# VectorE in written order through all four groups of layer 1

## The chip, the cores and the metric

The kernel runs on one core of a Trainium2 chip. The metric is the device time of one execution in microseconds (us); lower is better. The core has five engines, each with its own queue that it works through in order: TensorE (PE, matrix products; PEld is its weight load), VectorE (DVE, elementwise work), ScalarE (ACT, functions such as Ln and Exp), GpSimd (POOL) and SyncE (SP, which issues the transfers). They work side by side and wait for one another with semaphores. Which instruction stands ahead of which on one engine is fixed when the kernel is built.

## The reference

Sixteen graphs of 1024 nodes with 64 features share one adjacency matrix. Four layers follow one another, each of them `x = layernorm(x + layer(x))`. The change is in layer 1, which is, for each feature by itself, a softmax average over the neighbours:

```
feat   = softplus(x * (w0 / sqrt(2)) + b0)
scores = feat * wa + ba
attn   = softmax over neighbours j of scores[b, j, d]      # masked by adj
out    = sum over j of attn[b, i, j, d] * feat[b, j, d]
x      = layernorm(x + out)
```

Since a score depends on the neighbour and the feature alone, the average is a quotient of two products with the adjacency matrix: `adj @ (exp(scores) * feat)` over `adj @ exp(scores)`. Layers 0 and 2 are graph attention with one head, layer 3 has four heads; they enter here only where their work lies beside layer 1's.

## The kernel before

The 1024 nodes are eight blocks (`C = 8`) of 128, the graphs four groups (`NG = 4`) of four (`GB = 4`). All node features of a group lie in one SBUF tile, `x0` to `x3`. Layer 1 is a loop over the groups g, and inside it over the eight row blocks ic of the output.

*The product* (`product_l1`, L2008). For one row block TensorE adds up 16 products of 128 by 128 by 512 in one PSUM tile `po`: eight blocks of neighbours, each with a high and a low part (`hi`, `lo`) of the right side, which holds for four graphs both the exponentials and the exponentials times the features. The tiles `po` come from a pool of two buffers (L636), so the product of block n+2 can't start before the last reader of block n has done: L2027.

*The average* (`average`, L2019). ScalarE takes the logarithm of the denominators and the exponential of its negative, which is a first reciprocal `r` (L2022, L2023). VectorE improves it by one step and applies it (L2025, L2026, L2027), subtracts the quotient from `x` (L2030, the signs are turned so that this adds it) and takes the statistics of four rows (four L2032, into `st`). Each of these instructions reads what the one ahead of it wrote.

*The preparation of the next group* (`prep_l1`, L1862). A group has two halves q of two graphs each. Nine tasks are laid on the row blocks of the group before: ScalarE's softplus in four steps (L1870, L1873, L1877, L1880), VectorE's sum (L1883), eight transposes on TensorE (L1888, tile `pf`), VectorE's maximum (L1894, L1895, L1897) and ScalarE's exponential (L1898), eight transposes back (L1908, tile `pe`), then `hi` on ScalarE (L1910, L1916) and on VectorE the weighted features (L1911) and `lo` (L1912, L1917). The second L1917 of a half pair is the last thing that the next group's first product needs.

*The moments* (`moments`, L765). Behind a group's eight averages VectorE makes mean and variance out of `st` in seven rows (L771, 772, 773, 775, 776, 777 and L715, which keeps the largest variance). ScalarE takes the root (L718, L719), VectorE refines it in four rows (L723, 724, 725, 782), and ScalarE scales the group's 32 rows (L791, `scaled`). Root, refinement and scaling are a list `last`, of which the next group's loop runs one entry behind each average: `for task in last[ic : ic + 1] + ahead[ic]`. For group 0 this list holds what layer 0 has left over for its last graphs (L1125, L1130, L1150, L1158, L1163, L1164, L1171, moments, scaling). The list behind group 3 is run in layer 2.

*Layer 2's beginning*. From block 3 of group 2 on, the first tasks of layer 2 lie on the row blocks as well: transposes (L944), small products (L951, L998), and in group 3 eight masked exponentials `e` on VectorE (L1048).

*The order*. The loop is not wrapped in an order for TensorE, ScalarE or VectorE in groups 0 to 2: a planner in the language's layer decides there, by its own costs, how the instructions of an engine follow one another. In group 3 VectorE's instructions are kept in the order in which the program writes them (`tc.manual_schedule`), as those of all engines are in layers 0, 2 and 3.

Of the kernel before, what the change touches and what calls it, by code (L numbers as in the profile page):

```python
# [582 lines left out]
def fast_path(  # L583
# [26 lines left out]
    C = N // P  # L610
# [3 lines left out]
    GB = 4  # L614
    NG = B // GB
# [149 lines left out]
    def moments(st):  # L765


        n = st.shape[1]
        t = {k: small.tile([P, n], F32, tag=f"bn_{k}", name=f"bn_{k}") for k in ("mean", "d", "var", "rstd", "shift")}
        v = nc.vector  # L770
        v.tensor_tensor(t["d"], st[:, :, 1], st[:, :, 4], ALU.subtract)  # L771
        v.tensor_tensor(t["var"], st[:, :, 2], st[:, :, 5], ALU.add)
        v.tensor_tensor(t["mean"], st[:, :, 1], st[:, :, 4], ALU.add)

        v.scalar_tensor_tensor(t["d"], t["d"], 0.25, t["d"], ALU.mult, ALU.mult)
        v.tensor_scalar(t["var"], t["var"], 1.0 / D, LN_EPS, ALU.mult, ALU.add)
        v.tensor_tensor(t["var"], t["var"], t["d"], ALU.add)
        root, step = inverse_root(t["rstd"], t["var"])

        def finish():  # L780
            step()
            v.scalar_tensor_tensor(t["shift"], t["mean"], -0.5, t["rstd"], ALU.mult, ALU.mult)  # L782
            return t["rstd"], t["shift"]

        return root, finish

    def scaled(dst, src, moments, rows):

        rstd, shift = moments
        for c in rows:  # L790
            nc.scalar.activation(  # L791
                dst[:, c, :], src[:, c, :], AF.Identity,
                bias=shift[:, c : c + 1], scale=rstd[:, c : c + 1],
            )
# [1129 lines left out]
    with tc.tile_pool(name="ps_g", bufs=1, space=bass.MemoryType.PSUM, reuse_waits="tile") as ps_g, tc.tile_pool(  # L1924
# [66 lines left out]
        g=lambda: l1["psum"]("pg").rearrange("p (i c) q -> p i (c q)", i=2),  # L1991
# [11 lines left out]
    with tc.tile_pool(name="l1", bufs=2, reuse_waits="tile") as pool:  # L2003
        l1["halves"] = pool
        l1["psum"] = lambda name: ps_l.tile([P, C, P], F32, tag="l", name=name)
        aR = pool.tile([P, C, N], F32R, tag="aR", name="aR", bufs=1)

        def product_l1(g, ic):  # L2008
            po = ps_a.tile([P, 2, 2, P], F32, tag="acc", name=f"po{g}_{ic}")
            for k in range(C):  # L2010
                for e in (his[g], los[g]):
                    nc.tensor.matmul(  # L2012
                        po.rearrange("p q k f -> p (q k f)"), aR[:, k, ic * P : (ic + 1) * P],
                        e[:, k].rearrange("p q k f -> p (q k f)"),
                        start=(k == 0 and e is his[g]), stop=(k == C - 1 and e is los[g]),
                    )
            return po

        def average(g, ic, po, st):  # L2019

            r = pool.tile([P, 2, P], F32, tag="r1", name="r1", bufs=2)
            nc.scalar.activation(r, po[:, :, 1, :], AF.Ln)  # L2022
            nc.scalar.activation(r, r, AF.Exp, scale=-1.0)  # L2023
            t = pool.tile([P, 2, P], F32, tag="t1", name="t1", bufs=1)
            nc.vector.tensor_tensor(t, po[:, :, 1, :], r, ALU.mult)  # L2025
            nc.vector.scalar_tensor_tensor(r, t, 2.0, r, ALU.subtract, ALU.mult)  # L2026
            nc.vector.tensor_tensor(t, po[:, :, 0, :], r, ALU.mult)  # L2027
            y = xg[g][:, ic]
            yf = y.rearrange("p b d -> p (b d)")
            nc.vector.tensor_tensor(yf, yf, t.rearrange("p q f -> p (q f)"), ALU.subtract)  # L2030
            for b in range(GB):
                nc.vector.bn_stats(st[:, ic * GB + b, :], y[:, b, :])  # L2032

        ending[0]()
        for i, task in enumerate([l1_tasks[q][-2 + i] for q in range(2) for i in range(2)]):
            for k in range(2 * i, 2 * i + 2):
                (nc.scalar.copy if k % 2 else nc.vector.tensor_copy)(aR[:, k, :], aT[:, k, :])
            task()
        last = ending[1:]
        for g in range(NG):  # L2040
            ahead = [[] for _ in range(C)]
            for q in range(2 if g + 1 < NG else 0):

                for ic, task in zip((q, q, q, q, q + 1, q + 2, q + 2, q + 4, q + 5), prep_l1(g + 1, q)):
                    ahead[ic].append(task)
            places = {NG - 2: (3, 3, 4, 4, 5, 6, 7, 7), NG - 1: (0, 0, 0, 0, 0, 1, 2, 3, 4, 5, 6, 7)}.get(g, ())
            for ic, task in zip(places, l2_ahead[8 if g + 1 == NG else 0 :]):
                ahead[ic].append(task)
            st = (l1["both"] if g + 1 == NG else pool).tile([P, C * GB, 6], F32, tag="st1", name=f"st{g}")
            with ExitStack() as order:  # L2050
                if g + 1 == NG:
                    order.enter_context(tc.manual_schedule(engines={mybir.EngineType.DVE}))
                for ic in range(C):
                    po = product_l1(g, ic)
                    average(g, ic, po, st)
                    for task in last[ic : ic + 1] + ahead[ic]:
                        task()
            y = xg[g].rearrange("p c b d -> p (c b) d")
            mo = {}

            def spread_of(mo=mo, st=st):
                mo["root"], mo["end"] = moments(st)

            if g + 1 < NG:
                spread_of()

            def root(mo=mo):
                mo["root"]()

            def shift(mo=mo):  # L2070
                mo["n"] = mo["end"]()

            def rows(c, y=y, mo=mo):
                scaled(y, y, mo["n"], range(c * 8, c * 8 + 8))

            last = [spread_of] * (g + 1 == NG) + [root, shift] + [lambda c=c, rows=rows: rows(c) for c in range(C * GB // 8)]
    l3a = None

    def open_l3a():
# [128 lines left out]
    last = [(E, BURSTS + j, outs[E][1][0][3 * j : 3 * j + 3]) for j in range(3)]  # L2208
# [54 lines left out]
def kernel(tc, *args):  # L2263


    nc = tc.nc
    with tc.tile_pool(name="flag", bufs=1) as fp:
        redo = fp.tile([1, 1], I32, tag="redo", name="redo")
        fast_path(tc, redo, *args)
        again = nc.values_load(redo[0:1, 0:1], min_val=0, max_val=1)  # L2270
        with tc.If(again == 1):
            general_path(tc, *args)
# [32 lines left out]
```

## Time and profile before

| | |
|---|---|
| median of three runs | 1922.41 us (1922.39 to 1925.25) |
| the profiled execution's own time | 1922.41 us |
| its span, first to last instruction | 1920.4 us |
| layer 0, with loading | 0 to 265 us |
| hand-over to layer 1 | 265 to 279 us |
| layer 1 (first to last product) | 279 to 419 us |
| layer 2 | 419 to about 610 us |
| layer 3 | about 610 us to the end |
| first L2025 of groups 0, 1, 2, 3 | 287.87, 322.39, 356.90, 393.93 us |
| last L2025 of group 3 | 419.71 us |
| mean granted clock of TensorE | 0.99 |

The profile is taken from one execution. Its page gives the busy time of each engine and its share of the span, then the span in 40 slices with the busy share of each in tenths. A table by stretches gives, for each stretch of the span, busy microseconds and number of instructions of PE, PEld, DVE, ACT and POOL, the granted clock of TensorE (1.00 is full, 0.50 is half), the busy share of the transfer engines and GB/s. A line of waits reads: engine and line that waited, engine and line that ended the wait, microseconds in total, number of times, the longest. A line of the timeline reads: start, duration, engine, line, operation, written tile and read tiles with their shapes, and in brackets how long the engine was idle before it and what released it.

### The profile page before, as it was taken

Reading aid. Unit: us, or ns where it says so; the run is one execution under the profiler, and the core shown is the slowest. Engines: PE = TensorE matmul, PEld = TensorE weight load, DVE = VectorE, ACT = ScalarE, POOL = GpSimd, SP = SyncE. Lnnn points to the kernel's source line nnn. Section 1 sums busy time; section 2 is a strip of 40 time slices with the busy share of each in tenths; the row PEclk is TensorE's granted clock in tenths of the full one; section 3 lists DMA queues with packets and bytes.
Section 4 is the critical chain, followed back from the end, with each engine's and each line's share of the span. In section 5 each row is a group of like instructions: output and inputs, shape, how many; then the busy total and the mean of one; then the engine's idle time right before and its main releaser. Section 6 shows DMA issues by size and latency. Waiting matters only on the chain. (4 is left out here: it accounts for less than half of the span.)

```text
span 1920.4 us, 25705 instructions
## 1 busy us (share of the span) xinstructions
PE 1859.8 (97%) x9505; PEld 764.7 (40%) x9505; DVE 1753.8 (91%) x2924; ACT 1324.7 (69%) x2352; POOL 76.0 (4%) x77
## 2 busy tenths in 40 slices
PE   8999989999998999999999999999999999999996
PEld 4444347763333333333333333333333333333332
DVE  7899988899999888899998998999989899899997
ACT  4566568857879677676767767767676766776764
POOL 0000000000000000000000000000000000000001
PEclk8999989999999999999999999999999999999998
DMA  7000000000000300000001000010000100000000
GB/s 183 1 1 1 1 1 1 1 1 1 1 1 12 89 12 13 23 12 18 12 18 29 12 18 12 18 28 12 18 12 18 29 12 18 12 24 23 12 23 13
DMA packets 45746, 35.87 MB, mean 19 GB/s; under 512 B 37295, under 2 KB 37616, under 8 KB 45614
## 3 DMA queue, kind: packets, MB, share of 16 engines
q1 hardware_dynamic: 43534, 33.64, 6.8%
q8 instruction: 76, 1.25, 0.3%
q10 hardware_dynamic: 2080, 0.52, 0.1%
q14 instruction: 56, 0.46, 0.1%
HBM read 29.45 MB, written 4.70 MB: 18 GB/s over the span
## 5 line engine op out<-in xcount | busy, mean ns | idle before, releaser
L1450 ACT ACTIVATE e<-s,shift 128x1024 f32<-128x1024 f32 x512 | 538.9, 1123 | 240.5 <-PE s L1446 238.6
L1454 DVE TENSOR_TENSOR e<-e,aT 128x1024 f32<-128x1024 f32 x512 | 596.1, 1215 | 5.0 <-ACT e L1450 4.8
L1446 PE MATMUL s<-hT 64*128 64x512 f32 x2048 | 489.3, 602 | 2.5 <-ACT zT L1493 1.4
L1461 PE MATMUL y<-e,vals 128*64 128x512 f32 x2048 | 483.3, 599 | 1.9 <-DVE e L1454 1.0
L1446 PEld LDWEIGHTS s<-hT 64*128 64x128 f32 x2048 | 183.6, 185 | 288.0 <-issue 143.1
L1461 PEld LDWEIGHTS y<-e,vals 128*64 128x64 f32 x2048 | 135.2, 136 | 269.1 <-issue 200.1
L1048 DVE SCALAR_TENSOR_TENSOR e<-G_l,q,aT 128x1024 f32<-128x1024 f32 x150 | 185.7, 1278 | 0.2
L1630 DVE TENSOR_TENSOR e<-e,aT 128x1024 f32<-128x1024 f32 x128 | 156.3, 1225 | 11.2 <-ACT e L1617 1.6
L1060 PE MATMUL y_l<-e,vals_l 128*64 128x512 f32 x608 | 145.5, 605 | 2.3 <-DVE e L1048 2.3
L1622 DVE SCALAR_TENSOR_TENSOR junk<-e,aN 128x1024 bf16<-128x1024 f32 x120 | 146.1, 1217 | 0.0
L1617 ACT ACTIVATE e<-s,shift 128x1024 f32<-128x1024 f32 x128 | 138.6, 1114 | 2.4 <-PE s L1612 2.4
L1612 PE MATMUL s<-h2T 64*128 64x512 f32 x512 | 125.8, 591 | 0.0
L1638 PE MATMUL y<-e,h2v 128*64 128x512 f32 x512 | 125.6, 592 | 0.0
L2012 PE MATMUL po<-hi,aR 128*128 128x512 f32 x256 | 102.3, 400 | 10.5 <-ACT hi L1916 6.7
L1389 POOL PARTITION_ALL_REDUCE gtop<-top x48 | 52.9, 1101 | 1254.3 <-DVE top L1387 1046.9
L2012 PE MATMUL po<-lo,aR 128*128 128x512 f32 x256 | 100.5, 393 | 0.3 <-DVE lo L1917 0.3
L791 ACT ACTIVATE x<-m,bn_shift,bn_rstd 128x64 f32<-128x64 f32 x224 | 77.2, 428 | 15.7 <-DVE bn_shift L782 15.7
L1612 PEld LDWEIGHTS s<-h2T 64*128 64x128 f32 x512 | 50.1, 186 | 60.1 <-issue 37.3
L1493 ACT COPY zT<-poT 64x512 f32<-64x512 f32 x124 | 72.0, 581 | 1.1
L1060 PEld LDWEIGHTS y_l<-e,vals_l 128*64 128x64 f32 x608 | 38.6, 137 | 76.8 <-issue 61.0
L1468 ACT COPY yT<-y 128x512 f32<-128x512 f32 x64 | 38.5, 601 | 43.6 <-PE y L1461 42.6
L1638 PEld LDWEIGHTS y<-e,h2v 128*64 128x64 f32 x512 | 36.6, 137 | 73.6 <-issue 58.5
(299 smaller groups left out, 2144.4 us busy)
## 6 DMA issues: line engine op xcount, KB each, us to landing
r<-inverse SPq DMA_DIRECT2D x62, 256.0 KB
adj<-in_adj_dram SPq DMA_DIRECT2D x16, 512.0 KB
out_dram<-res SPq DMA_DIRECT2D x15, 256.0 KB
x<-in_x_dram SPq DMA_DIRECT2D x14, 256.0 KB
rows<-yT SPq DMA_DIRECT2D x62, 4.0 KB
x<-in_x_dram ACTq DMA_DIRECT2D x2, 256.0 KB
sums<-rows SPq DMA_DIRECT2D x31, 8.0 KB
inverse<-rt SPq DMA_DIRECT2D x31, 8.0 KB
```

Of the source, the lines that this page charges most:

```text
L1048: nc.vector.scalar_tensor_tensor(e, of_pair(b - b % 2, b % 2), pq[b - b % 2][1][:, k, b % 2 : b % 2 + 1], aT[:, k, :], ALU.max, ALU.mult,)
L1060: nc.tensor.matmul(held["y"][h * D : (h + 1) * D, :], vals[b][:, k, :], e[:, h * HALF : (h + 1) * HALF], start=(k == 0), stop=(k == C - 1),)
L1446: nc.tensor.matmul(s[:, i, :], hT[rows, k * P : (k + 1) * P], hT[rows, cols], start=True, stop=True)
L1450: nc.scalar.activation(e, s, AF.Exp, bias=shifts[b, n])
L1454: nc.vector.tensor_tensor(e, e, bc_mid(aT[:, k, h * HALF : (h + 1) * HALF], 2), ALU.mult)
L1461: nc.tensor.matmul(held[h][i * D : (i + 1) * D, :], vals[b][:, k, :], e[:, i, :], start=(k == 0), stop=(k == C - 1),)
L1612: nc.tensor.matmul(s[:, i, :], hT[rows, (i + k // CH) % 2, k % CH * P : (k % CH + 1) * P], hT[rows, 0, :], start=True, stop=True,)
L1617: nc.scalar.activation(e, s, AF.Exp, bias=shifts[b])
L1622: nc.vector.scalar_tensor_tensor(junk.rearrange("p c q -> p (c q)").bitcast(BF16), e.rearrange("p i q -> p (i q)"), 1.0, aN[:, k, :], ALU. ...
L1630: nc.vector.tensor_tensor(e, e, aT[:, k, :].rearrange("p (i q) -> p i q", i=2), ALU.mult)
L1638: nc.tensor.matmul(held["o"][h * D : (h + 1) * D, :], vals["out", b][:, k, :], e[:, h, :], start=(k == 0), stop=(k == C - 1),)
L2012: nc.tensor.matmul(po.rearrange("p q k f -> p (q k f)"), aR[:, k, ic * P : (ic + 1) * P], e[:, k].rearrange("p q k f -> p (q k f)"), start ...
```

## The change

The order that group 3 has is put on all four groups: VectorE's instructions of the whole loop over row blocks stand as the program writes them. And the moments of groups 0 to 2 are no longer written behind their own group. They become the first entry of the list `last`, as they were for group 3, so that they are written behind the first average of the next group, with root, refinement and each scaling one block later than before. No instruction is added or removed.

```diff
             st = (l1["both"] if g + 1 == NG else pool).tile([P, C * GB, 6], F32, tag="st1", name=f"st{g}")
-            with ExitStack() as order:
-                if g + 1 == NG:
-                    order.enter_context(tc.manual_schedule(engines={mybir.EngineType.DVE}))
+            with tc.manual_schedule(engines={mybir.EngineType.DVE}):
                 for ic in range(C):
                     po = product_l1(g, ic)
                     average(g, ic, po, st)
...
             def spread_of(mo=mo, st=st):
                 mo["root"], mo["end"] = moments(st)
 
-            if g + 1 < NG:
-                spread_of()
-
             def root(mo=mo):
                 mo["root"]()
...
-            last = [spread_of] * (g + 1 == NG) + [root, shift] + [lambda c=c, rows=rows: rows(c) for c in range(C * GB // 8)]
+            last = [spread_of, root, shift] + [lambda c=c, rows=rows: rows(c) for c in range(C * GB // 8)]
```

## The prediction

> **What bounds the kernel now.** I read the page first (busy shares, busy tenths), then the busy times by stage, then for layer 1 alone what TensorE waits for, and last VectorE's timeline there. The page, for one execution:
>
> ```profile
> PE 1859.8 (97%) x9505; PEld 764.7 (40%) x9505; DVE 1753.8 (91%) x2924; ACT 1324.7 (69%) x2352; POOL 76.0 (4%) x77
> PE   8999989999998999999999999999999999999996
> DVE  7899988899999888899998998999989899899997
> ```
>
> No engine is the bound everywhere, so the stage decides. Stretches of the span (columns: the stretch, its length, busy us and instructions of PE, PEld, DVE, ACT, POOL, granted clock, DMA): layer 0, its hand-over, layer 1, layer 2, layer 3.
>
> ```profile
> 0.00:265.00 265.00, 257.97 (x1696) 108.25 (x1696) 238.68 (x517) 142.53 (x377) 9.02 (x18) 0.98 0.14 34
> 265.00:279.00 14.00, 5.80 (x44) 5.04 (x40) 11.05 (x22) 13.70 (x24) 0.00 (x0) 0.77 0.01 2
> 279.00:419.00 140.00, 135.81 (x644) 110.12 (x644) 118.79 (x358) 108.98 (x246) 0.35 (x1) 0.99 0.00 1
> 419.00:610.00 191.00, 174.22 (x866) 72.02 (x864) 189.49 (x344) 148.09 (x503) 8.45 (x7) 0.98 0.01 4
> ```
>
> Layer 1 is TensorE's: 135.8 of 140 us, VectorE 118.8. Layer 2 is VectorE's: 189.5 of 191. So a delay of VectorE at the end of layer 1 is passed on whole, but for the 1.5 us that VectorE idles in layer 2. What TensorE waits for from 279 to 419:
>
> ```profile
> PE po L2012 <- DVE t L2027: 2.0, 2, 1.8
> PE po L2012 <- DVE top L1895: 1.8, 1, 1.8
> PE po L2012 <- DVE lo L1917: 0.3, 1, 0.3
> ```
>
> That is 4.1 us, and 3.8 of it (0.2, 1.81 and 1.80, inside the loop over groups) is all that a better order there could win. The end of group 0, on VectorE (start, us, line, operation):
>
> ```profile
> 313.69 0.41 DVE L2025 TENSOR_TENSOR t<-po,r 128x256 f32<-128x256 f32 x1
> 314.02 1.22 DVE L1917 TENSOR_TENSOR lo<-f,hi 128x1024 fp32r<-128x1024 f32 x1
> 315.15 0.42 DVE L2026 SCALAR_TENSOR_TENSOR r<-t,r 128x256 f32<-128x256 f32 x1
> 315.62 1.28 DVE L1894 TENSOR_SCALAR_CACHE_REDUCE t<-pf,wa 128x1024 f32<-128x1024 f32 x1
> 316.82 0.08 DVE L1894 DVE_READ_ACCUMULATOR t<-pf,wa 128x1 f32 x1
> 316.82 0.42 DVE L2027 TENSOR_TENSOR t<-po,r 128x256 f32<-128x256 f32 x1
> ```
>
> The average of row block 6 is taken apart. The last `lo` (L1917), which group 1's first product needs, is slipped in behind its first instruction and ends at 315.24. That product starts at 317.39, held by L2027 of block 6, which frees one of the two PSUM buffers, and not by `lo`.
>
> **What the change moves.** The order of the built program shows each average (L2025, 2026, 2027, 2030, four L2032) as one block. Seven moment rows (L771 to L715) move from the group's end to behind the next group's first average. The last L1917 of a half stands behind the whole of average 6. Instructions and their number stay. The orders of TensorE and ScalarE are planned anew inside layer 1; from layer 2 on all are as before. SP has no DMA in this stage and POOL one reduction for layer 2, whose ScalarE readers are done some 6 us before the first mask that needs them; both cost nothing, and one late reader would cost its lateness.
>
> In written order a group becomes a loop that nothing breaks: first average, VectorE's list up to the last `lo`, first product of the next group, Ln and Exp, first average. Its rows:
>
> 1. An average in one block: the starts 397.56, 398.02, 398.48, 398.94, 399.40 and the next at 399.92 give 2.36. (Mixed with other rows an instruction of it takes 0.34, not 0.46.) Seven of them: 16.5.
> 2. A half's preparation, start to start: L1883 1.14 to 1.19, L1894 with L1895 and L1897 1.62, L1911 1.13, L1912 1.16, L1917 1.15: 6.2. Two: 12.5.
> 3. Group 0 also holds the rest of layer 0: L1125, L1130 and two L1150 1.28, L1163 and L1164 1.33, eight L1171 1.16, seven moment rows 0.89, four step rows 0.73: 5.4.
> 4. Groups 1 and 2 hold instead seven moment rows of 32 columns, 1.2, and four step rows, 0.8: 2.0.
> 5. Behind the list: the product, 16 matmuls at 0.227 and a start, 3.68; L2022 0.38 and L2023 0.42 with hand-overs 0.13: 4.6 in all. VectorE has only average 7 (2.4) for it and then idles.
>
> *Group 0*: 16.5 + 12.5 + 5.4 + 4.6 = 39.1 from first average to first average. Before: 287.87 to 322.39 = 34.5. **+4.6.** I put ScalarE at no lateness here, since VectorE is never without work in this list.
>
> *Group 1*: 16.5 + 12.5 + 2.0 + 4.6 = 35.6, to which come 0.9 of waits for `hi` and `r` inside the list (L1911 waited 1.6 for `hi` once before) and ScalarE's lateness at the group's end. There the new order puts L1870 and L1873 of the next half right around Ln and Exp: 0 at least, 1.14 + 0.95 at most, 1.6 by following ScalarE's rows. 38.1 against 322.39 to 356.90 = 34.5. **+3.6**, from +2.0 to +4.1.
>
> *Group 2*: the same list with 1.2 of waits, ScalarE free at its end: 36.8. Before: 356.90 to 393.93 = 37.0, bound by TensorE, which has 24 further small products for layer 2 there. Its own sum (eight products 29.3, four sets of transposes 3.5, the others 3.9) is 36.7, so the two are level: **0**, from -0.3 to +1.5.
>
> *Group 3* was in written order already, with a product of 3.68 against an average and a mask, 2.36 + 1.24 = 3.60. The seven moment rows (1.04 in all) ran at 391.47, while VectorE waited for its first average; now they stand behind it, where 0.08 a block is free: **+1.2**, from 0 to +1.4.
>
> *The start*: the first L2025 was ready at 287.00 (end of L2023) but stood behind an L1883 until 287.87. ScalarE's L1158 (0.54) now comes later as well, so it starts near 286.4: **-1.5**.
>
> *ScalarE's scaling* (L791) of a group starts one block later. Its first reader, the transposes of x0 for layer 2 (L944), stands ahead of group 2's first product, which waits for `lo` anyway: nothing, unless ScalarE is over 2 us late.
>
> Sum: -1.5 + 4.6 + 3.6 + 0 + 1.2 = **+7.9 us**. Less what layer 2 can absorb, at most 1.5 by its idle time; I take 0, since the order of layer 2 has not changed and its rows follow one another.
>
> **TensorE's clock** comes on top, since the loop makes TensorE idle longer. What rows show (columns as above):
>
> ```profile
> 313.50:316.90 3.40, 2.08 (x14) 1.59 (x12) 3.35 (x9) 3.20 (x5) 0.00 (x0) 1.00 0.00 0
> 576.30:579.70 3.40, 1.58 (x8) 0.48 (x8) 3.33 (x14) 3.03 (x10) 0.33 (x1) 1.00 0.00 0
> 579.70:583.10 3.40, 3.40 (x12) 1.82 (x10) 3.33 (x9) 3.40 (x13) 0.00 (x0) 0.50 0.02 5
> 593.30:596.70 3.40, 3.40 (x12) 1.32 (x13) 3.40 (x4) 2.77 (x12) 0.00 (x0) 0.51 0.00 0
> ```
>
> A wait of 1.82 us at 576.6 was followed by 3.4 us at half clock, and so was one of 2.22 us; 1.81 at 315.6 was not. Half clock for 3.4 us costs a bound TensorE 1.7 us. In group 0 the list takes 34.5 us, and TensorE has 28.4 of its own beside it (seven products 25.8, four sets of transposes 3.5, less 0.9 for Ln and Exp): 6 us of waiting. Some 2 of them come in block 4 (transposes of `f`, whose L1883 stands behind L1171 and the moments) and some 4 at the end, but for one matmul; another 2 at the end of group 1. So none to four such windows: 0 to 6.8; I take one at the end of group 0, where the first product is on the loop: **+1.7**.
>
> The Trainium skill speaks on this ("TensorE: Matmul & The Clock Gate", HAM oscillation): the clock falls after an idle window of about 3.4 us. By that rule only the end of group 0 could be hit, an estimate of 0 or 1.7 us; the rows above show that half a window's wait can be enough, which would add up to two more.
>
> **+7.9 + 1.7 = +9.6.** The profiled execution took 1922.41 (span 1920.4 and 2.0 around it), which is the median of the runs shown: 1922.4 + 9.6 = **1932.0 us**.
>
> **Rivals.**
>
> *The loop doesn't bind: faster.* If the last `lo` were ready before product 7 ended, TensorE's 3.8 us of waits and the 1.5 at the start would go, and group 3 keep its +1.2: 1922.4 - 4.1 = 1918.3. For it: VectorE is at 118.8 of 140 in this stage. It decides at the list: group 1's period without waits is 34.5 - 1.8 = 32.7, less 4.6 leaves 28.1 us of list, and the rows come to 31.0 before any wait. Against it, then, by 3 us.
>
> *Half of it.* ScalarE is never late, no clock window falls, layer 2 absorbs its 1.5: -1.5 + 4.6 + 2.0 - 0.3 + 0.6 - 1.5 = +3.9, 1926.3. Against it: all ends together.
>
> *Heavier.* Three or four clock windows (6.0) and ScalarE late by the full 2.1 at the ends of groups 0 and 1 (2.1 and 0.5 more): +7.9 + 6.0 + 2.6 = +16.5, 1938.9. For it: ScalarE is newly planned, and the rows at 576 to 597 show how little it takes. Against it: a late TensorE gives VectorE time to catch up.
>
> *Not done at all*: excluded, the built order shows the blocks.
>
> **How the numbers follow.** Likeliest (7.9 with none, one or two windows, 1928 to 1935) 0.70; heavier 0.13; half 0.11; loop not binding 0.06. The range 1926.0 to 1937.5 leaves out the faster case and the far part of the heavier one. 0.2% (3.8 us) is about what a measurement of this kernel can tell from no change. Slower by more: 0.70 + 0.13 + half of 0.11 = 0.88; within: 0.06, since of the half case only its lower part is left; faster: 0.06.
>
> **What would show it.** Right: first L2025 of each group about 39, 38 and 37 us apart; at each group's first product TensorE waiting for `lo` (L1917), 4 us in group 0 and about 2 in group 1; after it VectorE idle some 2 us, released by L2023; a half-clock window near 320; layer 2 shifted as a whole. Wrong: groups still 34.5 apart, or `lo` done before product 7 ends; layer 2 shorter than 191 us by more than 1.5; or L2025 blocks of less than 2.3 us.

## The result, and the profile after

The changed kernel takes 1933.26 us (median; 1931.08 to 1935.20), the kernel before 1922.41 (1922.30 to 1925.25). The ratio is 1.0049, with a 95% interval of 1.0038 to 1.0061: half a per cent slower. The forecast was 1932.0 in a range of 1926.0 to 1937.5.

The profiled execution took 1935.2 us, its span is 1933.3, against 1920.4 before: 12.9 us more. First the page, busy times and two rows of the slices:

```profile
PE 1867.2 (97%) x9505; PEld 769.4 (40%) x9505; DVE 1757.3 (91%) x2924; ACT 1323.6 (68%) x2352; POOL 76.9 (4%) x77
PE   8999988999898999999999999999999999999996
DVE  6899978889999879799998998989989899899997
```

The shares are those of before; the page alone would not show that anything happened. The stretches do (the stretch, its length, busy us and instructions of PE, PEld, DVE, ACT, POOL, granted clock, DMA). Layer 1 now ends 13 us later, so its stretch runs to 432:

```profile
0.00:265.00 265.00, 258.21 (x1684) 109.18 (x1688) 237.27 (x513) 141.18 (x373) 9.10 (x18) 0.99 0.14 34
265.00:279.00 14.00, 7.21 (x56) 5.43 (x48) 9.76 (x19) 13.56 (x26) 0.00 (x0) 0.81 0.00 1
279.00:432.00 153.00, 143.18 (x645) 114.39 (x646) 125.11 (x364) 110.27 (x247) 0.35 (x1) 0.94 0.00 1
432.00:620.00 188.00, 169.64 (x846) 70.20 (x848) 186.49 (x340) 145.13 (x495) 8.45 (x7) 0.99 0.01 4
```

Layer 1 went from 140 to 153 us. TensorE's busy time rose by 7.4 there, with no instruction added, mostly because its clock fell from 0.99 to 0.94; its idle time rose from 4.2 to 9.8. Layer 2 is as full for VectorE as before, 186.5 of 188.

The starts of the first L2025 of each group, and of the last one, give the length of each group:

| us | first L2025 of group 0 | group 0 | group 1 | group 2 | group 3, to its last L2025 | from there to the span's end |
|---|---|---|---|---|---|---|
| before | 287.87 | 34.52 | 34.51 | 37.03 | 25.78 | 1500.7 |
| after | 287.87 | 42.16 | 38.83 | 37.01 | 26.60 | 1500.8 |
| after, another profile (below) | 290.20 | 40.05 | 37.98 | 37.01 | 26.58 | 1502.8 |

The whole difference of the first profile is made in groups 0 and 1 (+7.6 and +4.3), with 0.8 in group 3; nothing of it is given back in layers 2 and 3. What TensorE waits for from 279 to 432 us (engine and line that waited, who ended the wait, us in total, times, longest):

```profile
PE po L2012 <- ACT hi L1916: 8.4, 2, 6.2
PE po L2012 <- DVE lo L1917: 4.0, 3, 1.7
PE pf L1888 <- DVE f L1883: 1.9, 1, 1.9
PE po L2012 <- DVE t L2027: 0.7, 2, 0.4
```

The 6.2 of the first line lies at the hand-over, ahead of 280 us. The rest is at the group ends, but for the third line, which lies in the middle of group 0, and 0.3 us of the last, which lies in group 3. Here is the end of group 0 on VectorE, from the last `lo` on:

```profile
319.32 0.41 DVE L2025 TENSOR_TENSOR t<-po,r 128x256 f32<-128x256 f32 x1
319.77 0.43 DVE L2026 SCALAR_TENSOR_TENSOR r<-t,r 128x256 f32<-128x256 f32 x1
320.23 0.42 DVE L2027 TENSOR_TENSOR t<-po,r 128x256 f32<-128x256 f32 x1
320.69 0.43 DVE L2030 TENSOR_TENSOR x<-x,t 128x256 f32<-128x256 f32 x1
321.15 0.61 DVE L2032 BATCH_NORM_STATS2 st<-x 128x6 f32<-128x64 f32 x4
321.68 1.21 DVE L1917 TENSOR_TENSOR lo<-f,hi 128x1024 fp32r<-128x1024 f32 x1
...
330.03 0.42 DVE L2025 TENSOR_TENSOR t<-po,r 128x256 f32<-128x256 f32 x1 [4.79 <-ACT r L2023]
```

The average of block 6 now stands whole ahead of the `lo`, which ends at 322.89; before, it was taken apart and the `lo` ended at 315.24. Behind it VectorE has one average and then idles 4.8 us. TensorE at the same place:

```profile
321.01 0.49 PE L2012 MATMUL po<-hi,aR 128*128 128x512 f32 x1 [2.23 <-ACT hi L1916]
322.94 0.80 PE L2012 MATMUL po<-lo,aR 128*128 128x512 f32 x1 [1.43 <-DVE lo L1917]
323.53 0.63 PE L2012 MATMUL po<-hi,aR 128*128 128x512 f32 x1
323.96 0.63 PE L2012 MATMUL po<-lo,aR 128*128 128x512 f32 x1
```

It idles 2.23 us for `hi`, does one matmul, idles 1.43 for `lo`, and then goes at one matmul in 0.43 us, where 0.227 is the full pace. The granted clock in stretches of 3.4 us says the same:

```profile
318.10:321.50 3.40, 1.17 (x5) 0.41 (x3) 3.26 (x9) 3.40 (x9) 0.00 (x0) 0.99 0.00 0
321.50:324.90 3.40, 1.97 (x6) 1.57 (x6) 3.26 (x10) 3.40 (x5) 0.00 (x0) 0.50 0.00 0
324.90:328.30 3.40, 3.40 (x10) 2.63 (x9) 0.34 (x3) 2.04 (x3) 0.00 (x0) 0.50 0.00 0
359.00:362.40 3.40, 1.36 (x7) 0.78 (x5) 3.26 (x10) 3.40 (x6) 0.00 (x0) 1.00 0.00 0
362.40:365.80 3.40, 3.40 (x9) 2.62 (x8) 1.66 (x7) 3.40 (x4) 0.00 (x0) 0.50 0.00 0
```

Two stretches of half clock follow the end of group 0, and one the end of group 1.

### The profile page after: what moved, and what is told of

Same layout as the page of the kernel before. It is cut to its first block, busy times and chain, and to the rows that moved or that the text cites. A ratio compares the mean times of both kernels' runs of the same rounds, so it can differ in the third digit from the quotient of the medians.

```text
span 1933.3 us, 25707 instructions
## 1 busy us (share of the span) xinstructions
PE 1867.2 (97%) x9505; PEld 769.4 (40%) x9505; DVE 1757.3 (91%) x2924; ACT 1323.6 (68%) x2352; POOL 76.9 (4%) x77
```

## The experiments

The theory on record: a group is a closed loop of VectorE's *list* (from the group's first L2025 to the end of its last `lo`) and the *rest* (from there over the next group's first product and ScalarE's Ln and Exp to the next first L2025); the written order makes the list longer, and idle time of TensorE costs it its clock. The main rivals: that the moved moments cost something, that the place of the one `lo` costs it all, and that the clock costs nothing. Beside each run the kernel before was measured again (medians from 1924.4 to 1925.4 us), so it is the ratios that can be compared, not the times. In all kernels the list and the rest are worked out from VectorE's timeline:

| us | group 0: list | rest | group 1: list | rest |
|---|---|---|---|---|
| before | 27.4 | 7.2 | 25.6 | 8.9 |
| after, first profile | 35.0 | 7.1 | 31.8 | 7.1 |
| after, second profile | 33.9 | 6.1 | 31.8 | 6.2 |
| order alone | 33.9 | 6.2 | 31.1 | 5.3 |
| moments alone | 27.4 | 6.9 | 25.8 | 8.9 |
| order in groups 1 to 3 | 26.0 | 6.2 | 32.0 | 6.2 |
| extra matmuls | 33.9 | 4.8 | 31.7 | 6.2 |
| `lo` ahead | 32.2 | 7.8 | 30.0 | 7.0 |
| both, extra matmuls and `lo` ahead | 32.2 | 7.8 | 30.1 | 7.0 |
| without L1883 | 31.9 | 7.4 | 31.8 | 7.1 |
| `lo` and its transposes ahead, four buffers | 31.7 | 8.0 | 29.4 | 6.1 |
| rest of layer 0 first | 31.1 | 8.0 | 31.4 | 7.1 |
| before, `lo` and its transposes ahead, four buffers | 25.7 | 5.9 | 26.7 | 6.7 |
| before, `lo` and its transposes ahead, two buffers | 26.2 | 7.0 | 26.2 | 8.3 |

### Which of the two parts costs

The order alone, with the moments of a group behind their own group as before:

```diff
+            if g + 1 < NG:
+                spread_of()
...
-            last = [spread_of, root, shift] + [lambda c=c, rows=rows: rows(c) for c in range(C * GB // 8)]
+            last = [spread_of] * (g + 1 == NG) + [root, shift] + [lambda c=c, rows=rows: rows(c) for c in range(C * GB // 8)]
```

> VectorE in written order in all four groups, but the moments of groups 0 to 2 stay behind their own group. Theory (the loop from first average to last lo to first product): the order makes the loss. Group 0 (first L2025 to first L2025) stays at 42 us as in the changed kernel, its list is the same; groups 1 and 2 lose the seven moment rows from the list (1.2 us), since they now fall into the wait behind average 7: about 37.6 and 36.8; group 3 falls back to 25.8. Total about 1930.5 (1929 to 1932). Rival (the moved moments make the loss): 1922 to 1924, groups back at 34.5.

Measured: 1931.59 us, ratio 1.0032 (1.0021 to 1.0044). Groups 40.13, 36.39, 36.75, 25.76.

The moments alone, in the planner's order:

```diff
-            with tc.manual_schedule(engines={mybir.EngineType.DVE}):
+            with ExitStack() as order:
+                if g + 1 == NG:
+                    order.enter_context(tc.manual_schedule(engines={mybir.EngineType.DVE}))
```

> The other half alone: the moments behind the next group's first average, the planner's order in groups 0 to 2. Theory: the loop is not closed, since the last lo is still slipped into average 6; groups stay at 34.5, 34.5 and 37.0, group 3 takes the moment rows in: 1922.4 to 1924. Rival (the moved moments make the loss): 1930 or more.

Measured: 1923.86 us, ratio 0.9996 (0.9987 to 1.0006). Groups 34.29, 34.66, 37.03, 26.58. Most of the loss is that of the order (1.0032 of 1.0049), and without the order there is none. The moments by themselves cost 0.8 us in group 3 (26.58 against 25.78) and nothing that the time can tell; in written order group 1 is 1.6 us longer with them behind its first average than without (37.98 in the second profile of the changed kernel, 36.39 with the order alone).

### Which group

The changed kernel, with the planner's order in group 0:

```diff
-            with tc.manual_schedule(engines={mybir.EngineType.DVE}):
+            with ExitStack() as order:
+                if g:
+                    order.enter_context(tc.manual_schedule(engines={mybir.EngineType.DVE}))
```

> The changed kernel with the written order in groups 1 to 3 alone. Theory: group 0 falls back to 34.5 (from 42.2), its start is 1.2 later again, groups 1 and 2 stay at 38.8 and 37.0: 1933.3 - 7.7 + 1.2 = 1926.8 (1925 to 1928.5). Rival (the moved moments make the loss; group 0 holds layer 0's, which have not moved): no change, 1933.

Measured: 1926.48 us, ratio 1.0015 (1.0005 to 1.0025). Groups 32.24, 38.19, 37.07, 26.58. Group 0 falls by 7.8 from the 40.05 of the second profile, and group 1 keeps what it had. So each group's loss is its own; group 0 has the larger one. Group 0 is also 2.3 us shorter than in the kernel before, where the expectation had 34.5; why is open.

### The clock

The changed kernel, with 16 more matmuls of 256 columns at the ends of groups 0 and 1, whose result nobody reads:

```diff
+            if g < 2:
+                warm = ps_t.tile([P, HALF], F32, tag="t", name=f"warm{g}")
+                for k in range(16):
+                    nc.tensor.matmul(warm[:, : HALF // 2], aR[:, k % C, :P], his[g + 1][:, k % C, 0].rearrange("p k f -> p (k f)"), start=True, stop=True)
```

> The changed kernel with 16 extra matmuls of 256 columns (1.8 us) on TensorE between the last product of groups 0 and 1 and the first product of the next group, where TensorE waits anyway; they read the first half of the next group's hi, and their result is read by nobody. Theory (half-clock windows behind the waits at the ends of groups 0 and 1 are part of the loss): no half clock behind the first product of groups 1 and 2, that product back at 3.7 us from 6.2 and 5.3, so 2.5 and 1.6 us less: 1929 (1927.5 to 1930.5). Rival (the waits alone are the loss, VectorE catches up what the slow product costs): 1933, or more if the extra matmuls push the product out.

Measured: 1930.10 us, ratio 1.0029 (1.0018 to 1.0041). Groups 38.69, 37.91, 37.00, 26.58. The end of group 0 on TensorE:

```profile
317.99 2.07 PE L2059 MATMUL warm<-hi,aR 128*128 128x256 f32 x16
320.12 0.50 PE L2012 MATMUL po<-hi,aR 128*128 128x512 f32 x1
322.13 0.50 PE L2012 MATMUL po<-lo,aR 128*128 128x512 f32 x1 [1.51 <-DVE lo L1917]
322.47 0.40 PE L2012 MATMUL po<-hi,aR 128*128 128x512 f32 x1
322.71 0.40 PE L2012 MATMUL po<-lo,aR 128*128 128x512 f32 x1
```

The extra work fills the wait for `hi`, the wait for `lo` is as long as ever, and the product behind it runs at full pace. The list of group 0 is the same as in the second profile (33.9), the rest 4.77 in place of 6.13 or 7.14. So the clock is a cost of its own: 1.4 and 2.4 us of group 0 in the two profiles, and 0.8 of group 1 in the first. And it is not the main cause of the loss, which stays at 1.0029 without it (the intervals of 1.0029 and 1.0049 just overlap).

### The place of `lo`

The changed kernel, with the last task of a half, the weighted features and `lo`, one row block earlier, at blocks 4 and 5 in place of 5 and 6:

```diff
-                for ic, task in zip((q, q, q, q, q + 1, q + 2, q + 2, q + 4, q + 5), prep_l1(g + 1, q)):
+                for ic, task in zip((q, q, q, q, q + 1, q + 2, q + 2, q + 4, q + 4), prep_l1(g + 1, q)):
```

The expectation names the second half alone; the edit moves both.

> The changed kernel with the last task of a group's second half (ScalarE's hi and VectorE's lo, L1916 and L1917) laid on row block 5 in place of 6, so that the last lo stands ahead of average 6. Theory (the place of the last lo closes the loop): 2.4 us less of list in groups 0 and 1, and the clock windows at their ends go (2.5 and 1.6): 1926 to 1929. Rival (VectorE's list as a whole is full, so what is taken from in front of lo comes back as waits for hi or for PSUM): no gain, 1932 to 1935, with a late L2027 in place of a late lo.

Measured: 1933.45 us, ratio 1.0053 (1.0037 to 1.0070). Groups 39.94, 37.01, 37.64, 26.58. In the profile the edit takes 1.8 us from both lists and gives 1.7 and 0.8 back in the rest (against the second profile of the changed kernel). The rival is met, in its time and in its sign: in place of `lo`, TensorE now waits for another row of VectorE's, L2027 (two of its lines):

```profile
PE po L2012 <- DVE t L2027: 6.2, 4, 2.2
PE po L2012 <- ACT hi L1916: 6.2, 1, 6.2
```

The averages that `lo` was put ahead of now free their PSUM buffer later. And on VectorE the last `lo` can't go further forward, since its own input comes no earlier:

```profile
318.90 1.23 DVE L1917 TENSOR_TENSOR lo<-f,hi 128x1024 fp32r<-128x1024 f32 x1 [0.24 <-ACT hi L1916]
```

In the changed kernel `hi` was done at 320.96, and that last `lo` began at 321.68: a second chain, ScalarE's, ends only 0.7 us ahead of VectorE's.

Both edits together, the extra matmuls and the earlier `lo` (of both halves, though the expectation names the first alone):

```diff
-                for ic, task in zip((q, q, q, q, q + 1, q + 2, q + 2, q + 4, q + 5), prep_l1(g + 1, q)):
+                for ic, task in zip((q, q, q, q, q + 1, q + 2, q + 2, q + 4, q + 4), prep_l1(g + 1, q)):
...
+            if g < 2:
+                warm = ps_t.tile([P, HALF], F32, tag="t", name=f"warm{g}")
...
```

> The two edits of two earlier runs together: 16 extra matmuls at the ends of groups 0 and 1, and the weighted features and lo of a group's first half one row block earlier. With the extra matmuls alone TensorE still waited 2.8 us for lo (L1917) at three group ends, and the time was 1930.1 (1.0029). Theory that each wait is a cost of its own: lo goes, 2.8 us less, 1927 to 1928.5. Rival that the written order is one chain, in which the wait only takes another name (L2027, or ACT's hi): 1929.5 to 1931, with the lo wait replaced by one of L2027 of about the same sum.

Measured: 1932.27 us, ratio 1.0038 (1.0024 to 1.0051), which is 1929.7 on the median before; groups 39.95, 37.04, 37.65, 26.59, those of `lo` ahead by itself. The wait for `lo` is replaced by 2.5 us for L2027, the rival's case. But the run tells less than it was meant to: with `lo` earlier the planner puts the extra matmuls at 311.07, and the 2.16 us of waiting at 319 stay open and are followed by a half-clock stretch. Whether the two gains would add up isn't settled.

The changed kernel, with the last two tasks of each half (transposes back with `hi`, weighted features with `lo`) one row block earlier and the product's tiles taken from two pools in turn, so that L2027 holds no product:

```diff
-            po = ps_a.tile([P, 2, 2, P], F32, tag="acc", name=f"po{g}_{ic}")
+            at, tag = (ps_t, "t") if ic // 2 % 2 else (ps_a, "acc")
+            po = at.tile([P, 2, 2, P], F32, tag=tag, name=f"po{g}_{ic}")
...
-                for ic, task in zip((q, q, q, q, q + 1, q + 2, q + 2, q + 4, q + 5), prep_l1(g + 1, q)):
+                for ic, task in zip((q, q, q, q, q + 1, q + 2, q + 2, q + 3, q + 4), prep_l1(g + 1, q)):
```

> The changed kernel, with weighted features and lo one row block earlier in both halves and the product's PSUM tiles taken from two pools in turn, four buffers in place of two. On the kernel before the same two edits took every wait for L2027 and lo out of layer 1 and 2.7 us per group from groups 0 and 1 (31.6 and 33.4). Theory A, the written order costs only through those two waits: both gone here as well, groups of 32 to 34 us, a time of 1920 to 1923. Theory B, the written order is a chain through both engines, VectorE standing in line for ScalarE's r and hi with work ready behind: groups 0 and 1 stay at 37 to 40 us, 1928 to 1933, and VectorE idles for r and hi by 4 us a group or more.

Measured: 1935.86 us, ratio 1.0056 (1.0042 to 1.0070), which is 1933.2 on the median before, just above the range of theory B; theory A is out. Groups 39.76, 35.52, 39.08, 26.59. L2027 no longer holds a product, and TensorE waits 4.7 us for `lo` as before. Group 0's list is 2.2 us shorter than in the second profile, but its rest 1.9 longer, with 6.8 us of half clock and an L1873 of 1.05 between Ln and Exp on ScalarE. The idling for `r` and `hi` that theory B asked for, 4 us a group or more, isn't there: VectorE waits 3.3 us at the end of group 0, and in group 1 1.0 inside the list and 1.4 behind it. Group 1 does gain 2.5 us, more than theory B allowed; group 2 loses 2.1 of it, and layer 2 begins with 10 us of half clock.

### The length of the list

The changed kernel without VectorE's L1883 in groups 1 to 3, which takes two rows of 1.14 us out of the list:

```diff
-            nc.vector.tensor_tensor(h["f"], h["f"], h["t"], ALU.add)
+            if not g:
+                nc.vector.tensor_tensor(h["f"], h["f"], h["t"], ALU.add)
```

> The changed kernel without VectorE's L1883 in groups 1 to 3 (the logarithm is not added to the feature, so that the output of layer 1 lacks this term there): 1.15 us less, twice in each of the lists of groups 0 to 2, all else left. Theory (VectorE's list, one row behind the other, is the length of a group): 2.3 us less in group 0 and in group 1, nothing in group 2, which TensorE bounds: 1928.5 (1926.5 to 1930.5), groups at 39.9 and 36.5. Rival (the orders planned for TensorE and ScalarE set the length): 1932 to 1935.

Measured: 1933.19 us, ratio 1.0051 (1.0036 to 1.0066). Groups 39.31, 38.81, 36.99, 26.58. Group 0 loses 2.9 us against the first profile and 0.7 against the second; group 1's list is as long as with the two rows (31.76). The idle times of VectorE in that list (line numbers are one higher here):

```profile
333.21 0.42 DVE L2026 TENSOR_TENSOR t<-po,r 128x256 f32<-128x256 f32 x1 [1.18 <-ACT r L2024]
346.13 1.22 DVE L1912 TENSOR_TENSOR f<-f,pe 128x1024 f32<-128x1024 f32 x1 [1.73 <-ACT hi L1911]
```

In group 1 the 2.3 us came back as waits for ScalarE. In group 0 the list did become 2.0 us shorter, and the rest 1.3 longer, with 6.8 us of half clock against 3.4 in the second profile. The theory missed; the time is in the rival's range (the orders planned for TensorE and ScalarE set the length). No run keeps those two orders as they were before, so how much they add isn't shown. In a fixed order VectorE can't use them: what it could do in the meantime stands behind the waiting instruction.

The changed kernel, with the rest of layer 0 ahead of group 0's first average:

```diff
                     po = product_l1(g, ic)
+                    if g == 0 and ic == 0:
+                        for task in last[:3]:
+                            task()
                     average(g, ic, po, st)
-                    for task in last[ic : ic + 1] + ahead[ic]:
+                    for task in ([] if g == 0 and ic < 3 else last[ic : ic + 1]) + ahead[ic]:
```

> The changed kernel, with what layer 0 has left over (L1125 to L1171 and its moment rows) written ahead of group 0's first average in place of behind the first three. In the kernel before VectorE does these rows from 269 to 282 us; in the changed one they run at 290 to 300 us, inside the list, while VectorE idles 6.7 us ahead of its first L2025. Theory, that the list of group 0 is what was made longer: the list (first L2025 to the end of the last lo) 33.9 to 35.0 us becomes 28.5 to 30, group 0 40 to 42 becomes 34 to 36.5, the first average comes up to 1.5 us later because L1163 and L1164 stand ahead of a lo, group 1 keeps 37.9 to 38.8, and the time is 1927 to 1930. Rival, that a shorter list only gives the wait another name, as with the two earlier edits to the list: group 0 38.5 us or more, 1931 to 1934.

Measured: 1933.29 us, ratio 1.0055 (1.0041 to 1.0068). Groups 39.11, 38.41, 37.08, 26.60. The edit did what it says: the rows are done by 282.5 us, in the gap ahead of the first average at 286.95, and VectorE is busy for 28.6 us of the list in place of 32.5. But the list only falls to 31.1, since VectorE now waits 1.1 us in it for ScalarE's `r` and `hi`, and the rest grows to 8.0. At the end of group 0 TensorE waits again, first for `hi`:

```profile
316.20 0.51 PE L2012 MATMUL po<-hi,aR 128*128 128x512 f32 x1 [1.85 <-ACT hi L1916]
318.11 0.79 PE L2012 MATMUL po<-lo,aR 128*128 128x512 f32 x1 [1.41 <-DVE lo L1917]
```

and on ScalarE that `hi` (L1916) stands behind the scaling of layer 0's rows, which in written order come behind VectorE's four step rows at block 4:

```profile
312.79 2.43 ACT L791 ACTIVATE x<-m,bn_shift,bn_rstd 128x64 f32<-128x64 f32 x7
315.11 1.04 ACT L1916 CAST hi<-f 128x1024 fp32r<-128x1024 f32 x1
```

In the kernel before, ScalarE had done that scaling by 296 us. The theory's 34 to 36.5 for group 0 missed, the rival's 38.5 or more met; but here too 6.8 us of half clock (316.8 to 323.6) follow the waits, twice those of the second profile.

### A version that beats both

The two edits that help TensorE, put on the kernel before, in the planner's order: the last two tasks of each half one block earlier and four buffers for the product.

```diff
-            po = ps_a.tile([P, 2, 2, P], F32, tag="acc", name=f"po{g}_{ic}")
+            at, tag = (ps_t, "t") if ic // 2 % 2 else (ps_a, "acc")
+            po = at.tile([P, 2, 2, P], F32, tag=tag, name=f"po{g}_{ic}")
...
-                for ic, task in zip((q, q, q, q, q + 1, q + 2, q + 2, q + 4, q + 5), prep_l1(g + 1, q)):
+                for ic, task in zip((q, q, q, q, q + 1, q + 2, q + 2, q + 3, q + 4), prep_l1(g + 1, q)):
```

> The kernel before, with two things: the last three tasks of a half one row block earlier (back at q + 3, weighted at q + 4), and the products' PSUM tiles taken from two pools of two buffers in turn (row blocks 2, 3, 6, 7 from the pool that layers 0 and 2 use), so that a product waits for L2027 of four blocks before. Theory (TensorE has 3.8 us of waits in layer 1 in the kernel before, and VectorE enough room as long as its rows may be mixed): the three waits of 0.2, 1.8 and 1.8 go, 4 us less: 1918.4 (1917 to 1920). Rival (VectorE is full there too): no change, 1922.

Measured: 1919.71 us, ratio 0.9980 (0.9970 to 0.9990). Groups 31.62, 33.41, 37.27, 25.76. All waits of TensorE for L2027, L1895 and `lo` in layer 1 are gone. The end of group 0 on VectorE, for comparison with the one above (lines are one higher from L2010 on):

```profile
312.49 1.21 DVE L1917 TENSOR_TENSOR lo<-f,hi 128x1024 fp32r<-128x1024 f32 x1
313.88 0.42 DVE L2026 TENSOR_TENSOR t<-po,r 128x256 f32<-128x256 f32 x1 [0.19 <-ACT r L2024]
314.34 0.42 DVE L2027 SCALAR_TENSOR_TENSOR r<-t,r 128x256 f32<-128x256 f32 x1
314.80 0.43 DVE L2028 TENSOR_TENSOR t<-po,r 128x256 f32<-128x256 f32 x1
315.14 1.22 DVE L1883 TENSOR_TENSOR f<-f,t 128x1024 f32<-128x1024 f32 x1
```

The `lo` is done at 313.7, ahead of two averages and of an L1883 that is for the group after next. The earlier tasks by themselves, with two buffers:

```diff
-                for ic, task in zip((q, q, q, q, q + 1, q + 2, q + 2, q + 4, q + 5), prep_l1(g + 1, q)):
+                for ic, task in zip((q, q, q, q, q + 1, q + 2, q + 2, q + 3, q + 4), prep_l1(g + 1, q)):
```

> The first of the two alone: the kernel before with back at q + 3 and weighted at q + 4, two PSUM buffers. Theory (waits for a buffer and for lo are two waits, and both must go): part of the gain, 1920.3 (1919 to 1922). Rival (the buffer is what counts): 1922.4, groups at 34.5.

Measured: 1922.10 us, ratio 0.9987 (0.9977 to 0.9996); groups 33.26, 34.49, 36.12, 25.77. The earlier tasks give 1.3 us in group 0, nothing in group 1 and 0.9 in group 2; with the four buffers it is 2.9 and 1.1, and group 2 is 0.2 longer. The intervals of the two ratios overlap, so this split rests on one profile each.

### The changed kernel once more

No edit; the kernel of the change as it stands.

> The changed kernel as it stands, beside the next two, so that they have a measure from the same chip. Both theories: 1933.3 us, from 1931.5 to 1935, a ratio of about 1.0045 to the kernel before; the number of half-clock windows in layer 1 may differ from execution to execution, two to four of them.

Measured: 1935.02 us, ratio 1.0052 (1.0038 to 1.0066). Its profile is the second one of the tables. It has one half-clock stretch in layer 1 (324.0 to 327.4) where the first profile had four, and 3 us less in layer 1; but five in layer 2 where the first has one, and from the last L2025 to the end it takes 2 us longer. The sum comes out nearly the same. One stretch in layer 1 is less than the two to four expected.

## Why the prediction was right

**The start** (-1.5). VectorE now waits for `r` ahead of its first L2025, as said, in place of an L1883:

```profile
287.87 0.43 DVE L2025 TENSOR_TENSOR t<-po,r 128x256 f32<-128x256 f32 x1 [6.69 <-ACT r L2023]
```

The start itself, 287.87, is the very number of before, but in an execution whose layer 0 ran later. Measured from layer 0's last L1111, before and in the first profile after, the size can be told:

```profile
267.84 1.11 PE L1111 MATMUL po<-l_wd,yT_l 64*128 64x64 f32 x16
269.14 1.11 PE L1111 MATMUL po<-l_wd,yT_l 64*128 64x64 f32 x16
```

That is 20.03 us before and 18.73 after, and 18.73 again in the second profile (271.47 to 290.20): -1.3. In the other runs it is 20.0 wherever group 0 has the planner's order, and 18.7 to 19.2 wherever it has the written one.

**Group 0** (39.1 by rows, 40.8 with one clock window). Measured 42.16 and 40.05. The list was put at 34.5 and took 33.9 in the second profile, 35.0 in the first, where one of its half-clock stretches (304.4 to 307.8) lies inside the list. The rest was put at 4.6 and 1.7 for the clock: 6.13 and 7.14 were measured, and 4.77 with the extra matmuls, so the clock took 1.4 and 2.4. VectorE idles 4.79 and 3.78 us at the end, where the sign was "some 2"; less what the clock took, it is 2.4 both times.

**Group 1** (38.1). Measured 37.98 in the second profile: a list of 31.75 against 31.9, and 6.23 against 4.6 + 1.6 behind it. The 1.6 for ScalarE's lateness was read from the order of its rows, and in the rows of the second profile L1877 and L1873 do stand ahead of and between Ln and Exp:

```profile
365.43 1.26 ACT L1877 ACTIVATE f<-x,b,c 128x1024 f32<-128x1024 f32 x1
366.56 0.39 ACT L2022 ACTIVATE r<-po 128x256 f32<-128x256 f32 x1
366.82 1.08 ACT L1873 ACTIVATE t<-t 128x1024 f32<-128x1024 f32 x1
367.77 0.43 ACT L2023 ACTIVATE r<-r 128x256 f32<-128x256 f32 x1
```

The first profile has 38.83, by the stretch of half clock at 362.4.

**Group 2** (0). 37.01 in both profiles, against 37.03. **Group 3** (+1.2): +0.8. The seven moment rows found a little more room than the 0.08 us a block allowed. **Layer 2** (absorbs nothing): 1500.8 against 1500.7.

**The clock** (one window, +1.7). One in the second profile. The first had four, in three places, and its groups 0 and 1 are 3.0 us longer, 2.9 of it where the stretches lie (1.1 in group 0's list, 1.0 and 0.8 in the two rests). None to four was the span given.

Without the start, the terms sum to 11.1 us for layer 1; the two profiles grew by 12.8 and 9.8. That the forecast came within 1.3 us of the median is partly luck: with the clock's stretches the two profiles of one kernel differ by 3 us in layer 1.

What the prediction's own reading could not show, and the experiments did: it named the last `lo` as what TensorE would be held by, put ScalarE at no lateness in group 0, and the profile's list of waits seems to agree. But the first 2.2 us of that wait at the end of group 0 name `hi`, which is done only 0.7 us before VectorE comes to the last `lo`. Taking `lo` forward moved the wait to L2027; the other edits to the list left it with `hi` or `lo`. And though they took 1.8 to 2.8 us out of group 0's list (against the second profile), nothing came off the time (1.0051 to 1.0056, against 1.0049 and 1.0052).

The second chain is not the only reason for that; the clock is another. The rest of group 0 in the second profile, with the extra matmuls, and with the rest of layer 0 first:

```profile
324.13:330.26 6.13, 6.08 (x20) 4.92 (x21) 2.22 (x9) 4.76 (x6) 0.00 (x0) 0.74 0.00 0
322.08:326.85 4.77, 4.72 (x21) 3.87 (x22) 2.21 (x8) 4.67 (x6) 0.00 (x0) 1.00 0.00 0
318.06:326.06 8.00, 7.95 (x24) 6.31 (x25) 2.22 (x9) 5.59 (x7) 0.00 (x0) 0.65 0.00 0
```

Without L1883 and with four buffers the granted clock is 0.65 there as well. TensorE works nearly throughout, so the rest times its clock is an estimate of the rest at full clock: 4.5 us in the second profile, where 4.8 were measured with the extra matmuls, and 4.8 to 5.2 in the three runs at 0.65. With their lists of 31.1 to 31.9, group 0 would take 36 to 37 us at full clock, against the 38.7 measured with the extra matmuls. So it isn't shown that a shorter list wins nothing; what is shown is that in these three runs it won 0.3 to 0.9 us of group 0 while half clock twice as long followed the wait. No run has both the shorter list and the full clock.

What the written order moved can be counted. Before, VectorE did most of the rest of layer 0 and two L1883 between 269 and 288 us, ahead of group 0's first average, and most of the average of block 6 behind the last `lo`; and ScalarE had its scaling done early. In written order VectorE's list grows from 24.2 to 32.6 us of work in group 0 and from 20.7 to 29.6 in group 1. That the loss is the sum of these rows, and not also the new orders of TensorE and ScalarE, is argued, not shown.

A step that was costed at nothing and was not quite: ScalarE's scaling. The prediction has it one block later by the list and looked at its readers in layer 2; what it stands ahead of on ScalarE, the last `hi`, was not looked at. In group 0 it is layer 0's scaling, whose place in the list the change leaves alone; the written order holds back VectorE's four step rows that it needs, so that it is done by 296 us before and ends at 320 us after, just ahead of the last `hi` (319.92). With VectorE's list as long as it is, it costs little; once the list was made shorter, it was next. How much group 0 would gain if the scaling were moved as well wasn't tried.

The rival on the other side (the loop doesn't bind, 1918.3) is near what the planner's order reaches with `lo` earlier and four buffers, 1919.7 (1918.6 on the median before): that is the time with TensorE's waits gone. The written order didn't lead there.

## What to carry to other kernels

Where an engine's list has the planner's order, look at what that order does in the gaps ahead of the first result and behind the last one that another engine needs; a written order pays for each row that it pulls from there into the loop. When a wait goes and its time stays, look for a second chain that ends less than a microsecond ahead of the first (here `hi` on ScalarE, 0.7 us), and at the granted clock behind the wait, which can eat what the edit gave; change both, or give the engines more slack (buffers, an earlier task) in the order that there is.

## What the runs showed of the hardware

The Trainium skill ("TensorE: Matmul & The Clock Gate", HAM oscillation) has as its rule that TensorE should have no gap above about 3.4 us. Here TensorE was never idle for so long in the loop, and stretches of half clock followed waits of 1.87 us (at 303.36), of 2.23 and 1.43 (at 321 and 323), and of 1.66 (at 361.86). The measurement decides: about half of such a gap can be enough. It need not be: the second profile has 1.85 us in the place of the 1.87 and the same 1.66, and no fall behind either.

What sorts these is TensorE's busy time in a stretch of 3.4 us. The changes of the clock in the first profile (304.4, 307.8, 321.5, 328.3, 362.4, 365.8) lie whole multiples of 3.41 us apart, to a tenth. In the stretches of layer 1 cut at such points, 0.51 (second profile), 1.17, 1.36 and 1.53 us (first profile) were followed by half clock, and 1.55 and 1.92 (second profile) and 2.06 (extra matmuls) were not. So the same wait counts or doesn't by where it lies in the stretch. Close to 1.5 us the profiles don't tell a sharp threshold.

Nor does every fall of the clock have an idle stretch ahead of it. In the second profile of the changed kernel, at the beginning of layer 2, all of TensorE and then L951 alone (PE and PEld, clock, DMA):

```profile
433.20:436.60 3.40, 3.40 (x24) 2.33 (x24) 3.36 (x8) 1.81 (x9) 0.00 (x0) 1.00 0.00 0
436.60:440.00 3.40, 3.40 (x10) 0.90 (x8) 3.33 (x11) 0.93 (x5) 0.43 (x1) 0.50 0.00 0
433.20:436.60 3.40, 2.11 (x16) 1.94 (x16) 1.00 0.00 0
```

TensorE has no gap in the 3.4 us, by its modelled ends, and then goes at half clock. But 2.11 us of them are 16 matmuls of only 4 columns (L951, 128x4); without these it would be busy for 1.3 us, as ahead of other falls. The runs without L1883 and with the rest of layer 0 first have 2.11 us of L951 in that place too, and the same fall; the first profile has 1.94, the order in groups 1 to 3 1.98, the order alone 1.90, and no fall. The margin is thin; it looks as if matmuls of 4 columns hardly count as work for the clock, but no run tests it. With `lo` ahead and four buffers in written order, half clock lasted 10 us at a stretch (431.3 to 441.5), behind a wait of 2.23 us; TensorE was busy throughout, 3.4 of the first 6.8 us with L951. Two executions of one kernel differ by 3 us in layer 1 and by 2 in layer 2, along with the number of such stretches, so a difference of that size between two profiles proves nothing; the ratios with their intervals do.
